# Low halves of loaded weights: the second operand of the subtraction moved from SBUF to a PSUM copy

## The chip, the cores and the metric

The kernel runs as one program on one core of a Trainium2 chip. The engines are named as the profile names them: PE is TensorE (PEld its weight loads), DVE is VectorE, ACT is ScalarE, POOL is GpSimd, SP is the engine whose queue issues most of the DMAs. The metric is the device time of one execution in microseconds. A profile describes one execution of its own, whose span is a few microseconds off the median of the timed runs.

## The reference

Two cross-attention layers with image tokens, over 16 sequences of 256 tokens and 320 channels (20 heads of 16). The context has 256 tokens of 512 channels; its last 4 tokens are image tokens. Cut to what matters (layer 0; layer 1 differs in how the image scores are normalised):

```python
q = x @ Wq;  k = text @ Wk;  v = text @ Wv
text_out = softmax(q_h @ k_h.T * scale) @ v_h
ip_k = ip @ Wk_ip;  ip_v = ip @ Wv_ip
fused = q_h @ ip_k_h.T * scale + 0.5 * sem          # sem: what the text attention reads, against ip
ip_out = (softmax(fused) * spatial_mask) @ ip_v_h
x = (text_out + ip_out) @ Wout + bout + x
```

Everything is float32. The kernel makes every product of two float32 matrices from a high half (the value rounded to the format that TensorE takes at full rate) and a low half (the value less its high half), and multiplies high by high, high by low and low by high.

## The kernel before, in words

The work runs in slots, one for each group of four heads of each sequence: 80 slots of layer 0 (five a sequence), then 80 of layer 1. A slot makes the scores (line 701 into the bank pair S), their row maxima on DVE (lines 702 and 703, tile `mn`), a turn of the maxima into rows by a small matmul (line 708) and a DMA, the transposed scores (line 723 into the banks T), their exponent on ACT (line 726, tiles `P`), a product with the image part on POOL (line 729), and the product with the values (line 766 into the bank P). In layer 1 the same places have lines 865, 867, 884, 859, 879, 895 (POOL), 904/905 (norms) and 916/926.

Between these, `fill` runs the steps of other tasks at set times: keys, queries, values, projections, and the loading of weights. The order of TensorE is the order in which the program is written; ACT, DVE, POOL and SP are ordered by the framework's scheduler, within limits that `queued` and `anchor` set.

What the change touches is `halves` (line 153): it rounds a source into `hi` with an ACT copy (line 158) and subtracts that from the source for `lo` (line 161), on DVE unless told otherwise. It is called with `loaded=True` for pieces that a DMA has brought into a raw tile in SBUF (`rawc` or `raw`, two buffers each), through `in_turn`. On DVE that is 31 pieces:

- the context of sequences 2 and 3, four pieces of 128x512 (`cta`, `ctb`), between 58 and 67 us of the span;
- the output weights of layer 0, three pieces of 128x320 (`wF`), from 85 to 99 us;
- the image tokens of all sequences, 128x256 (the `kst<-rawc` row), at 526 us, and the five weights of layer 1 that follow until 631 us: `wki1` (four `wB` pieces of 384), `wk1` (four of `wA`), `wv1` (four of `wC`, 320), `wvi1` (three `wB` of 512), `wq1` (three of `wE`, 384);
- the context of sequence 2 for layer 1 (two pieces of 512) at 722 us, and the output weights of layer 1 (three of 320) from 731 to 740 us.

A piece laid out by heads needs three subtractions (260, 4 and 60 columns, from `rounded`), an output weight two (256 and 64), the others one. The other contexts have their low halves made on POOL, and a source that TensorE made is in PSUM already; neither is touched.

`bank()` hands out the general PSUM banks, called X, in a ring of three, in the order in which the program asks for them. Whoever is given a bank waits until every reader of the tile that had it three requests earlier is done. `maxima0` (line 708), the projections, keys, values and semantic scores all take their banks from this ring.

Of the kernel before, what the change touches and what calls it, by code (L numbers as in the profile page):

```python
# [18 lines left out]
H = 20  # L19
HP = 24  # L20
D = 16
# [29 lines left out]
def xattn2(  # L51
# [27 lines left out]
    nc = tc.nc  # L79
# [11 lines left out]
    def bank(tag="X"):  # L91
        return ps.tile([128, 512], F32, tag=tag, name=tag, bufs=BANKS[tag])
# [60 lines left out]

    def halves(hi, lo, src, eng=nc.vector, loaded=False):
        order = queued if loaded else lambda inst: inst
        if len(hi.shape) != len(src.shape):
            src = src.rearrange("p (d h) -> p d h", d=D)[:, :, :H]
        order(nc.scalar.copy(hi, src))
        for to, *at in lo if isinstance(lo, list) else [(lo,)]:
            at = (slice(None), *at)  # L160
            order(eng.tensor_sub(to, src[at], f(hi)[at]))
# [22 lines left out]
    def in_turn(parts, wait, tag="raw", eng=nc.vector):  # L184

        ahead, parts, tags = [], list(parts), tag.split()
        for i in range(len(parts) + 1):
            if len(tags) > 1:
                new = () if i else range(len(parts))
            else:  # L190
                new = range(i + 1 if i else 0, min(i + 2, len(parts)))
            if i:
                halves(*ahead.pop(0), eng, wait)
            for j in new:
                src, hi, lo = parts[j]
                raw = buf(tags[j // 2 % len(tags)], [128, 512], bufs=2)
                shape = src.shape
                raw = raw[:, : shape[1]] if len(shape) == 2 else raw.rearrange("p (k n) -> p k n", k=shape[1])
                dma(raw, src)
                ahead.append((hi, lo, raw))  # L200
            if wait:
                yield
# [57 lines left out]
    def evacuate(hi, lo, out, m):  # L260

        if m < 2:
            return halves(hi, lo, out)
        hi, lo = hi[:64], lo[:64]
        both = buf("both", list(hi.shape), bufs=2)
        nc.scalar.copy(hi, out[:64])
        nc.scalar.copy(both, out[64:])
        nc.vector.tensor_sub(out[:64], out[:64], f(hi))
        nc.vector.tensor_add(lo, out[:64], both)  # L269
# [102 lines left out]
    def weights1():  # L372


        cipn = buf("rawc", [128, 512], bufs=2, name="cipn")[:BI]
        dma(cipn, cip_d)
        yield
        sq = buf("rawc", [128, 512], bufs=2, name="sq")[:BI]
        nrm = rn[:BI, 0:1]
        nc.scalar.activation(sq, cipn, AF.Square, accum_out=nrm)  # L380
        yield
        nc.gpsimd.tensor_scalar_max(nrm, nrm, EPS2)
        nc.gpsimd.memset(rn[:BI, 1:2], -0.5)
        nc.gpsimd.tensor_tensor(nrm, nrm, rn[:BI, 1:2], op=ALU.pow)
        yield
        dg = buf("rawc", [128, 512], bufs=2, name="dg")[:BI]
        nc.gpsimd.memset(dg[:, BI : BI + 128], 1.0)
        nc.scalar.activation(dg[:, :BI], ident[:BI, :BI], AF.Copy, scale=nrm)
        yield
        rp = bank()  # L390
        mm(rp[:, :BI], dg[:, BI : BI + 128], dg[:, :BI], start=True, stop=True)
        nc.vector.tensor_copy(rn, rp[:, :BI])
        cip = w1["cip"] = buf("kst", [128, 2, 4, BI], FR, bufs=SIZES["KST"], name="cip")
        raw = buf("rawc", [128, 4, BI], bufs=2, name="cipT")
        dma(raw, cipT_d.rearrange("(k p) n -> p k n", p=128))
        yield
        halves(cip[:, 0], cip[:, 1], raw, nc.vector, True)
        w1["loads"] = started(weights_by_row(wki1_d, 0.3, RAWS))
        yield
# [917 lines left out]
    for c in range(B // 2):  # L1317
        n, k = 10 * c, [("k0", c)] if c else []
# [14 lines left out]
    for b in range(B):  # L1333
        n = NS + 5 * b
# [340 lines left out]
```

## Time and profile before

| | |
|---|---|
| time, median of 3 runs | 1478.3 us (1476.85 to 1479.2) |
| time of the profiled execution | 1483.24 us |
| its span | 1481.5 us |
| busy: PE, POOL, DVE, ACT | 96%, 82%, 77%, 61% of the span |

"Busy" is the share of the span in which an engine had an instruction of its own running; an engine that waits for a semaphore is idle, but one whose instruction has been issued and is held up inside counts as busy. The page's second part cuts the span into 40 slices of 37 us; PE stands at 9 tenths nearly everywhere. The table of stretches gives the same for any stretch, with the clock that TensorE was granted (1.00 is full speed). In a row of the timeline, `x3` means that so many instructions were merged, and the brackets at its end hold the time for which the engine stood idle before the first, and what ended it.

### The profile page before, as it was taken

What the parts mean: (1) busy time and instruction counts of PE and PEld (TensorE: products, weight loads), DVE (VectorE), ACT (ScalarE), POOL (GpSimd) and SP (SyncE); (2) the same over time, 40 slices, a digit from 0 to 9 for tenths busy, and PEclk for the clock granted to TensorE, in tenths of its full rate; (3) what the DMA queues carried; (4) which work ended last, traced back from release to release, by engine and by line L of the source; (5) the groups of instructions that cost most, each with busy time, mean ns of one, the idle gap of its engine ahead of it and who ended that gap; (6) DMA issues with size and microseconds to landing.
All of it is one profiled execution on the core that took longest, in us unless ns stands there. A gap on an engine that the chain in (4) does not pass through costs nothing.

```text
span 1481.5 us, 35836 instructions
## 1 busy us (share of the span) xinstructions
PE 1418.0 (96%) x12578; PEld 1147.1 (77%) x12578; DVE 1133.5 (77%) x2527; ACT 897.5 (61%) x2173; POOL 1217.7 (82%) x1590
## 2 busy tenths in 40 slices
PE   8889999999999989789999999999999999999998
PEld 7778888888888878567778777877787777777765
DVE  6567777777777788867878888788878878887886
ACT  6346565656565645546666676666766766676663
POOL 6259898989999978889678888788878888888885
PEclk8899999999999999989999999999999999999999
DMA  7766777776777665765444444444444444533401
GB/s 241 199 205 202 214 209 214 204 213 193 229 205 219 201 202 160 198 201 157 138 105 124 126 135 110 125 140 120 116 119 138 121 116 120 147 114 93 125 25 51
DMA packets 229118, 232.43 MB, mean 157 GB/s; under 512 B 38186, under 2 KB 198860, under 8 KB 228940
## 3 DMA queue, kind: packets, MB, share of 16 engines
q1 hardware_dynamic: 226736, 229.18, 54.2%
q8 instruction: 100, 1.64, 0.5%
q10 hardware_dynamic: 2204, 0.97, 0.3%
q14 instruction: 78, 0.64, 0.1%
HBM read 117.65 MB, written 77.07 MB: 131 GB/s over the span
## 4 chain that ended last, share of the span: by engine, by line
PE 69%; POOL 10%; DVE 9%; DMA 4%; ACT 3%; issue 3%; SPq 1%; ACTq 0%; DVEq 0%; POOLq 0%
PE X L904 14%; PE X L247 14%; PE P L766 6%; PE X L567 6%; PE S L701 5%; PE P L916 4%; PE P L926 4%; PE T L723 4%; POOL wt L895 3%; PE T L859 3%; PE S L865 3%; POOL P L729 3%; PE X L257 2%; DMA qs<-qd 2%; PE X L570 1%
## 5 line engine op out<-in xcount | busy, mean ns | idle before, releaser
L729 POOL TENSOR_TENSOR P<-P,rs 128x512 f32<-128x512 f32 x320 | 408.1, 1304 | 80.4 <-ACT P L726 79.7
L895 POOL TENSOR_TENSOR wt<-P,ctb 128x512 f32<-128x512 f32 x316 | 402.4, 1293 | 39.8 <-ACT ctb L894 39.3
L904 PE MATMUL X<-ctb,gm 128*128 128x512 f32 x1106 | 295.4, 400 | 4.5 <-DVE wt L905 4.5
L726 ACT ACTIVATE P<-T 128x512 f32<-128x512 f32 x320 | 175.8, 594 | 178.7 <-PE T L723 135.3
L905 DVE TENSOR_TENSOR wt<-X,wt 128x512 f32<-128x512 f32 x320 | 217.3, 683 | 35.8 <-PE X L904 28.0
L904 PEld LDWEIGHTS X<-ctb,gm 128*128 128x128 f32 x1106 | 194.1, 189 | 39.1 <-DVE wt L905 7.9
L879 ACT ACTIVATE P<-T 128x512 f32<-128x512 f32 x320 | 173.2, 593 | 79.6 <-PE T L859 76.6
L894 ACT ACTIVATE ctb<-P 128x512 fp32r<-128x512 f32 x316 | 182.4, 626 | 14.9 <-PE X L904 13.6
L867 DVE TENSOR_REDUCE mn<-S 128x4 fp32r<-128x1008 f32 x160 | 191.2, 1195 | 0.0
L703 DVE TENSOR_REDUCE mn<-S 128x4 fp32r<-128x716 f32 x160 | 142.6, 891 | 0.0
L766 PE MATMUL P<-P,vr 128*32 128x256 f32 x1920 | 128.6, 390 | 2.7 <-POOL P L729 1.9
L701 PE MATMUL S<-ks,qs 125*128 125x256 f32 x640 | 118.1, 308 | 10.2 <-DVE mn L703 4.7
L701 PEld LDWEIGHTS S<-ks,qs 125*128 125x128 f32 x640 | 88.9, 195 | 46.9 <-issue 28.1
L723 PE MATMUL T<-qs,ks 127*128 127x256 f32 x640 | 106.0, 289 | 0.2 <-ACT P L726 0.2
L777 DVE STREAM_TRANSPOSE nt<-P 128x512 f32<-128x512 f32 x80 | 57.2, 715 | 52.2 <-PE P L766 51.3
L702 DVE TENSOR_REDUCE mn<-S 128x4 fp32r<-128x308 f32 x160 | 74.4, 465 | 28.5 <-PE S L701 28.2
L766 PEld LDWEIGHTS P<-P,vr 128*32 128x32 f32 x1920 | 56.2, 111 | 47.3 <-POOL P L729 7.7
L723 PEld LDWEIGHTS T<-qs,ks 127*128 127x128 f32 x640 | 90.6, 195 | 1.1 <-ACT P L726 0.6
L926 PE MATMUL P<-wt,zone 128*32 128x256 f32 x1280 | 85.3, 379 | 0.7 <-DVE wt L905 0.7
L916 PE MATMUL P<-P,v1t 128*32 128x256 f32 x1280 | 85.9, 385 | 0.0
L247 PE MATMUL X<-wC,cta 128*128 128x324 f32 (+1 forms) x480 | 79.9, 313 | 0.3 <-DVE kst L269 0.3
L865 PE MATMUL S<-ks,qs 48*128 48x256 f32 x640 | 74.5, 309 | 3.9 <-DVE mn L867 2.5
(389 smaller groups left out, 2999.3 us busy)
## 6 DMA issues: line engine op xcount, KB each, us to landing
qd<-q SPq DMA_DIRECT2D x96, 256.0 KB
qs<-tph SPq DMA_DIRECT2D x64, 308.0 KB
qs<-qd SPq DMA_DIRECT2D x80, 192.0 KB
ks<-kd SPq DMA_DIRECT2D x80, 192.0 KB
ks<-kd SPq DMA_DIRECT2D x160, 96.0 KB
qs<-qd SPq DMA_DIRECT2D x160, 96.0 KB
kd<-kst SPq DMA_DIRECT2D x57, 256.0 KB
ks<-M SPq DMA_DIRECT2D x64, 215.4 KB
```

The source lines that it names most:

```text
L247: last = mm(out, lhs(a, k), rhs(b, k), start=i == 0, stop=i == len(terms) - 1)
L701: mm(sp[:, h], Q[: XROW + T0, h, t * 128 : (t + 1) * 128], K[: XROW + T0, h], start=True, stop=True)
L723: mm(st[p][:, j], K[:KS0, 2 * p + j, t * 128 : (t + 1) * 128], Q[:KS0, 2 * p + j], start=True, stop=True)
L726: exp = anchor(nc.scalar.activation(pt, st[p], AF.Exp, scale=SCALE))
L729: anchor(nc.gpsimd.tensor_mul(pt, pt, rs[:, t : t + 1].to_broadcast([128, 2, S])))
L766: mm(pv[32 * s : 32 * s + 32, o : o + S], v[:, vt, h : h + 32], P[k, s // 2][:, t, s % 2], start=vt < 2, stop=vt != 1,)
L867: anchor(nc.vector.tensor_reduce(mn[:, :, t], sp[:, :, :T1], axis=AX.X, op=ALU.max))
L879: anchor(nc.scalar.activation(P[k, u][:, t], st[u], AF.Exp, scale=SCALE))
L894: nc.scalar.activation(R[k, u][:, t], P[k, u][:, t], AF.Copy, scale=0.5)
L895: anchor(nc.gpsimd.tensor_sub(W[k, u][:, t], P[k, u][:, t], f(R[k, u][:, t])))
L904: mm(yp, gm[:, gb], R[k, u][:, kt], start=i == 0, stop=i == len(blocks[n]) - 1)
L905: w1["wt"] = nc.vector.tensor_mul(W[k, u][:, n], yp, W[k, u][:, n])
```

## The change

For a loaded piece whose low half DVE makes, ACT first copies the whole raw piece into a general PSUM bank. The subtraction then reads that copy, and no longer the raw tile. The high half is still rounded from the raw tile in SBUF.

```diff
     def halves(hi, lo, src, eng=nc.vector, loaded=False):
         order = queued if loaded else lambda inst: inst
+        if loaded and eng is nc.vector:
+            n = 1
+            for d in src.shape[1:]:
+                n *= d
+            there = bank()[: src.shape[0], :n]
+            if len(src.shape) == 3:
+                there = there.rearrange("p (k n) -> p k n", k=src.shape[1])
+            order(nc.scalar.copy(there, src))
+        else:
+            there = src
         if len(hi.shape) != len(src.shape):
-            src = src.rearrange("p (d h) -> p d h", d=D)[:, :, :H]
+            src, there = [t.rearrange("p (d h) -> p d h", d=D)[:, :, :H] for t in (src, there)]
         order(nc.scalar.copy(hi, src))
+        src = there
         for to, *at in lo if isinstance(lo, list) else [(lo,)]:
             at = (slice(None), *at)
             order(eng.tensor_sub(to, src[at], f(hi)[at]))
```

ACT has 31 instructions more, and TensorE's order stays as it was. In the changed program the lines behind this place have numbers higher by 11: the new copy is line 163, the rounding 168, the subtraction 172.

DVE at the first piece of the output weights of layer 0, from the reciprocal of one slot on (`q_0` is the tile of the queries of the next sequence, `wF_0` the weight, `X_` a general bank). Before:

```order
L780 RECIPROCAL P_69<-nt_1_131 128x16
L161 TENSOR_TENSOR wF_0_998<-rawc_0_126,wF_0_998 128x256
L161 TENSOR_TENSOR wF_0_998<-rawc_0_126,wF_0_998 128x64
L781 TENSOR_TENSOR P_69<-P_69,mk_101 128x8
L161 TENSOR_TENSOR wF_0_998<-rawc_1_127,wF_0_998 128x256
L161 TENSOR_TENSOR wF_0_998<-rawc_1_127,wF_0_998 128x64
L161 TENSOR_TENSOR q_0_161<-X_972,q_0_161 128x256
L783 TENSOR_TENSOR tmp_1_818<-nt_1_131,P_69 128x256
L268 TENSOR_TENSOR X_983<-X_983,kst_0_182 64x2x179
```

After, on the same engine at the same place:

```order
L791 RECIPROCAL P_69<-nt_1_131 128x16
L792 TENSOR_TENSOR P_69<-P_69,mk_101 128x8
L794 TENSOR_TENSOR tmp_1_826<-nt_1_131,P_69 128x256
L172 TENSOR_TENSOR q_0_161<-X_980,q_0_161 128x256
L279 TENSOR_TENSOR X_991<-X_991,kst_0_182 64x2x179
L172 TENSOR_TENSOR wF_0_1006<-X_1024,wF_0_1006 128x256
L172 TENSOR_TENSOR wF_0_1006<-X_1024,wF_0_1006 128x64
```

The subtractions of the weight read a bank now, and the low half of the queries stands ahead of them, where it stood behind four of them.

ACT at the context of sequences 2 and 3, from its first piece to the maxima of slot 2 (`mt`) and their DMA. Before:

```order
L158 CAST cta_0_77<-rawc_0_126 128x512
L726 ACTIVATE P_0_122<-T_67 128x512
L726 ACTIVATE P_1_123<-T_68 128x512
L158 CAST cta_1_78<-rawc_1_127 128x512
L158 CAST ctb_0_79<-raw_693 128x512
L158 CAST ctb_1_80<-raw_695 128x512
L654 ACTIVATE rs_1_133<-X_755 128x512
L710 CAST mt_0_598<-X_767 16x128
L726 ACTIVATE P_2_124<-T_67 128x512
```

After:

```order
L163 COPY X_730<-rawc_0_126 128x512
L168 CAST cta_0_77<-rawc_0_126 128x512
L737 ACTIVATE P_0_122<-T_67 128x512
L737 ACTIVATE P_1_123<-T_68 128x512
L163 COPY X_763<-rawc_1_127 128x512
L168 CAST cta_1_78<-rawc_1_127 128x512
L168 CAST ctb_0_79<-raw_693 128x512
L168 CAST ctb_1_80<-raw_695 128x512
L163 COPY X_767<-raw_693 128x512
L665 ACTIVATE rs_1_133<-X_757 128x512
L163 COPY X_771<-raw_695 128x512
L721 CAST mt_0_598<-X_775 16x128
```

Four copies stand among the roundings and exponents, and the bank of the maxima, `X_775`, is the one that the copy `X_763` had.

ACT at the image values of layer 1 (`wvi1`), from an exponent to the maxima (`sp_1` holds the semantic scores of one half of a sequence, made by TensorE into a bank). Before:

```order
L726 ACTIVATE P_1_123<-T_68 128x512
L158 CAST wB_7664<-rawc_1_127 128x512
L158 CAST wB_7665<-rawc_0_126 128x512
L625 COPY sp_1_391<-X_7653 128x77
L710 CAST mt_0_598<-X_7677 16x128
```

After:

```order
L737 ACTIVATE P_1_123<-T_68 128x512
L163 COPY X_7711<-rawc_1_127 128x512
L168 CAST wB_7704<-rawc_1_127 128x512
L163 COPY X_7717<-rawc_0_126 128x512
L168 CAST wB_7705<-rawc_0_126 128x512
L636 COPY sp_1_391<-X_7693 128x77
L645 ACTIVATE sp_0_390,mx_0_394<-sp_0_390,mx_0_394 128x77
L721 CAST mt_0_598<-X_7721 16x128
```

Two copies stand ahead of the semantic scores, and the two banks that they take bring the bank of the maxima, `X_7721`, round to the one that these scores, `X_7693`, had.

## The prediction

> **What bounds the kernel now.** I read the page first, then the table of stretches, then TensorE's rows with the waits ahead of them, and last what DVE and POOL did in those waits.
>
> ```profile
> span 1481.5 us, 35836 instructions
> PE 1418.0 (96%) x12578; PEld 1147.1 (77%) x12578; DVE 1133.5 (77%) x2527; ACT 897.5 (61%) x2173; POOL 1217.7 (82%) x1590
> ...
> 57.00:70.00 13.00, 9.21 (x66) 6.54 (x65) 8.11 (x10) 5.40 (x12) 7.54 (x7) 0.85 0.78 198
> 83.00:95.00 12.00, 10.32 (x77) 9.41 (x79) 8.56 (x20) 5.45 (x14) 4.55 (x6) 0.86 0.75 228
> 520.00:635.00 115.00, 95.88 (x865) 78.89 (x865) 97.14 (x209) 60.11 (x151) 91.20 (x97) 0.96 0.66 183
> 718.00:745.00 27.00, 24.32 (x217) 18.54 (x210) 23.46 (x46) 16.09 (x37) 13.77 (x20) 0.94 0.47 143
> ...
> 745.00:1380.00 635.00, 631.40 (x5617) 492.41 (x5617) 515.48 (x1102) 427.34 (x1018) 530.97 (x818) 1.00 0.44 122
> ```
>
> A row of stretches gives its length, then PE, PEld, DVE, ACT and POOL busy, TensorE's clock, and the DMA's share and rate. TensorE is the bound: in 635 us of layer 1 it is idle for 3.6 us. The four stretches in which weights are loaded are the exception: of 167 us TensorE works 139.7, idle for 27.3 us, and its clock is below 1 in all four. Only there can the change win.
>
> Why, the clearest case shows:
>
> ```profile
> 526.23 4.24 DVE L161 TENSOR_TENSOR kst<-rawc,kst 128x256 fp32r<-128x256 f32 x1
> 526.44 2.53 POOL L729 TENSOR_TENSOR P<-P,rs 128x512 f32<-128x512 f32 x2
> 528.93 1.26 POOL L556 TENSOR_TENSOR ho<-hT,ho 128x512 fp32r<-128x512 f32 x1
> 531.50 0.23 PE L708 MATMUL X<-ident_r,mn 128*16 128x128 f32 x1 [2.68 <-DVE kst L161]
> ```
>
> A subtraction of 256 columns with both operands in SBUF lasts 4.24 us and ends at 530.47, just behind the third of three POOL instructions (530.19); DVE was held for as long as POOL kept going. TensorE stood for 2.68 us behind it.
>
> **What DVE gets back.** The first two rows give the time of everything that touches `rawc`, and `raw`, summed over the load stretches; DVE's part is the 59 subtractions. The next four are subtractions that no POOL work met, the last those with a PSUM operand.
>
> ```profile
> sum 160.00, PE 0.43 PEld 0.29 DVE 32.74 ACT 10.05 POOL 0.00; mean PE 0.05 PEld 0.04 DVE 4.09 ACT 1.26 POOL 0.00
> sum 160.00, DVE 14.67 ACT 5.01 POOL 0.00; mean DVE 1.83 ACT 0.63 POOL 0.00
> ...
> 549.08 0.62 DVE L161 TENSOR_TENSOR wB<-raw,wB 128x260 fp32r<-128x260 f32 x3
> 87.08 0.55 DVE L161 TENSOR_TENSOR wF<-rawc,wF 128x256 fp32r<-128x256 f32 x2
> 593.45 0.47 DVE L161 TENSOR_TENSOR wC<-raw,wC 128x320 fp32r<-128x320 f32 x1
> 722.20 1.28 DVE L161 TENSOR_TENSOR cta<-rawc,cta 128x512 fp32r<-128x512 f32 x2
> ...
> L161 DVE TENSOR_TENSOR q<-X,q x62: 411/425/427, 32.8 to 1372.8; 128x256 fp32r<-128x256 f32 x62
> ```
>
> Now 32.74 + 14.67 = 47.4 us. Unheld: 11 pieces of 384 at 0.62 (6.8), six of 320 in two parts at 0.55 (3.3), four of 320 at 0.47 (1.9), nine of 512 at at most 0.68 (6.1), one of 256 at 0.41 (0.4): 18.5 us. That a PSUM operand leaves DVE unheld, the last row shows: 62 subtractions all over a run in which POOL is 82% busy, none over 0.427 us. So DVE gets 28.9 us back; the bounds are 0 (still held) and 28.9, and I take 28.9 because the row is the same instruction.
>
> [...]
>
> **What of that TensorE gets back.** These are its waits in the load stretches (with the one at 531.50), two DVE rows behind them, and one stretch.
>
> ```profile
> 63.68 0.56 PE L247 MATMUL X<-ctb,wA 128*128 128x156 f32 x3 [1.11 <-DVE ctb L161]
> 66.58 0.71 PE L247 MATMUL X<-ctb,wA 128*128 128x156 f32 x2 [2.34 <-DVE ctb L161]
> 88.02 0.77 PE L247 MATMUL X<-cta 128*77 128x192 f32 x6 [1.36 <-DVE q L161]
> 542.22 0.51 PE L567 MATMUL X<-ho,wF 128*128 128x256 f32 x2 [0.80 <-POOL ho L557]
> 576.29 0.22 PE L708 MATMUL X<-ident_r,mn 128*16 128x128 f32 x1 [1.75 <-DVE mn L703]
> 596.55 0.34 PE L623 MATMUL X<-kb,q 128*128 128x156 f32 x1 [1.07 <-DVE q L269]
> 601.61 0.22 PE L708 MATMUL X<-ident_r,mn 128*16 128x128 f32 x1 [1.51 <-DVE mn L703]
> 610.67 0.34 PE L642 MATMUL X<-ident,sp 128*77 128x128 f32 x1 [2.66 <-ACT sp L638]
> 626.15 1.50 PE L766 MATMUL P<-P,vr 128*32 128x256 f32 x24 [0.57 <-DVE tmp L783]
> 628.91 0.74 PE L701 MATMUL S<-ks,qs 125*128 125x256 f32 x4 [1.26 <-DVE mn L703]
> 632.37 0.23 PE L708 MATMUL X<-ident_r,mn 128*16 128x128 f32 x1 [2.24 <-DVE mn L703]
> 741.33 0.50 PE L865 MATMUL S<-ks,qs 48*128 48x256 f32 x4 [2.51 <-DVE mn L867]
> ...
> 571.51 2.58 DVE L161 TENSOR_TENSOR wA<-raw,wA 128x260 fp32r<-128x260 f32 x3 [1.11 <-ACT wA L158]
> 736.63 3.03 DVE L161 TENSOR_TENSOR wF<-rawc,wF 128x256 fp32r<-128x256 f32 x2 [1.38 <-ACT wF L158]
> ...
> 615.00:630.00 15.00, 10.97 (x102) 8.08 (x102) 13.04 (x26) 6.82 (x15) 15.00 (x15) 1.00 0.65 176
> ```
>
> Without the one that names POOL they sum to 21.1 us. By stage, with what is late next:
>
> - Context at 58 us (3.45): DVE's gain is eaten by ACT. The first piece lands at 58.9; four copies, four roundings, two exponents and one other stand in a row, 8 x 0.57 + 2 x 0.54 + 0.6 = 6.3 us, to 65.2. With a subtraction of 0.68 the last low half is there at 65.9 instead of 66.5. Take **0.7**.
> - `wF` (1.36): in the order shown above the queries' subtraction no longer stands behind four of the weight's. Take **1.2**.
> - Image tokens (2.68): 4.24 becomes 0.41, but POOL's rows end at 530.19 all the same, and the wait at 542.22 is for POOL. Take **1.7**.
> - `wk1` (1.75): 2.58 becomes 0.62 ahead of the reduction waited for. Take **1.6**. `wv1` (1.07): **0.7**.
> - `wvi1` (1.51 and 2.66): **0**, since the third order shown puts a new wait here (priced below).
> - `wq1` (4.07): three pieces shrink, but POOL works all 15 us of 615 to 630. Take **2.5**.
> - `wo1` (2.51): 3.03 becomes 0.55. Take **2.2**.
>
> That is 10.6 us. To it comes the clock:
>
> ```profile
> 88.00:93.40 5.40, 5.07 (x28) 4.79 (x29) 2.43 (x7) 0.84 (x3) 0.46 (x1) 0.69 1.03 302
> 526.00:536.00 10.00, 7.16 (x66) 5.71 (x64) 7.94 (x12) 3.38 (x10) 5.47 (x8) 1.00 0.66 202
> 632.80:636.20 3.40, 3.40 (x20) 3.17 (x23) 1.64 (x3) 1.42 (x4) 3.40 (x5) 0.50 0.75 203
> 741.00:745.40 4.40, 4.07 (x18) 3.59 (x19) 3.41 (x8) 1.31 (x4) 0.63 (x3) 0.61 0.47 146
> ```
>
> After the waits at 88, 632 and 741 TensorE runs at half clock for 3.4 us, 1.7 us lost each time, 5.1 in all; after the one at 531.50 it does not. Bounds 0 and 5.1; I take the middle, **2.5**. [...]
>
> **What it costs.** The trace has no ACT copy from SBUF into PSUM; the nearest rows are the roundings, SBUF to SBUF.
>
> ```profile
> 58.90 0.62 ACT L158 CAST cta<-rawc 128x512 fp32r<-128x512 f32 x1 [1.35 <-DMA rawc<-in_cT_dram]
> 601.14 1.13 ACT L158 CAST wB<-rawc 128x512 fp32r<-128x512 f32 x2
> ...
> L729 POOL TENSOR_TENSOR P<-P,rs 128x512 f32<-128x512 f32 x320 | 408.1, 1304 | 80.4 <-ACT P L726 79.7
> ```
>
> 31 copies at 0.62 at most are 19 us, on an engine that is idle for 80 of the 167 us. All hidden is 0, all on the path 19. A copy ahead of an exponent delays POOL, which waits for exponents 0.25 us a piece (80.4 over 320): a dozen such copies at 0.25 are 3 us, my value, near the lower end because ACT is half idle. The cover for the rest is this idle time. Queued behind a copy on ACT are exponents, evacuations of banks and the DMAs of the maxima; TensorE and POOL wait for those. For the shorter ring elsewhere I add 1 us. SP only sees raw tiles come free a little sooner, as ACT and no longer DVE is their last reader: 0. Sum: 10.6 + 2.5 - 4 = **9.1 us** less. The profiled execution took 1483.24 us and would take 1474.1; it stands 4.9 above the median, from which I subtract the same: **1469.2 us**.
>
> **Rivals.** *All waits go*: 21.1 + 5.1 less a few for ACT, about 24, so 1454; for it speaks that DVE is named in nearly every wait, against it POOL's full 15 us. *The gain goes to the next late engine*: TensorE comes sooner and waits for POOL or ACT; 1 us left, 1477. For it speaks the 82% of POOL, against it TensorE's near absence of idle time from 745 us on, with the same POOL load. *The ring* (slower): a copy takes one of three banks, and TensorE, in order, stands at its third request behind a subtraction or an evacuation. The place is `wvi1`: two copies, 1.13 us as the roundings, push the semantic scores back, and the bank of the maxima waits for their addition, so that TensorE goes on near 603.7 instead of 601.6, 2.1 us lost. If ten of the copies do that, 21 us go against 13.1: 1486. It decides from 13.1 / 31 = 0.42 us a copy on. Against it speaks that elsewhere products of a microsecond lie between the copies. *It doesn't do what it says*: DVE stays held and 4 us are added, 1482; the 62 rows speak against it.
>
> **How the numbers follow.** Forecast (1462 to 1475) 0.61; all waits 0.14; next engine 0.14; ring 0.09; not as said 0.02. A measurement of this kernel tells about 0.2%, 3 us, from no change. Faster takes the first two, 0.75; same the third, 0.14; slower the last two, 0.11. The range, 1458 to 1479, holds all of the first and third and about a third of the second; it leaves out most of 'all waits' and the slower ones.
>
> **What would show it.** Right: the subtractions sum to about 18.5 us, none much over 0.7; the waits at 531, 576, 632 and 741 shrink below half, and the half-speed stretches behind the last two go. Wrong: rows of line 172 that still end with POOL's; copies well over 0.62 us; TensorE's maxima (line 719) or norms waiting for line 172 or 637; or the same idle time now named POOL or ACT.

## The result and the profile after

| | before | changed |
|---|---|---|
| median, timed side by side | 1478.3 us of 5 runs (1474.32 to 1481.74) | 1468.9 us of 5 runs (1465.03 to 1472.39) |
| ratio, with its 95% interval | | 0.9929 (0.9905 to 0.9954) |
| profiled execution and its span | 1483.24, 1481.5 us | 1465.03, 1463.2 us |

The kernel became faster by 9.4 us, 0.6%, and the interval leaves out 1; forecast were 9.1. The profiled executions lie 18.2 us apart, because the one before is 4.9 us above its median and the one after 3.9 below: what the two traces show by stage is more than the change is worth, and the experiments have to say which part of it repeats.

The first lines of the page after give the span and the busy times:

```profile
span 1463.2 us, 35841 instructions
PE 1409.4 (96%) x12578; PEld 1139.1 (78%) x12578; DVE 1108.8 (76%) x2527; ACT 909.4 (62%) x2204; POOL 1211.6 (83%) x1590
```

The view of the cores gives the mean clock that TensorE was granted (0.983 in the profile of before):

```profile
core 0: 1463.2 us, clock 0.992
```

DVE is busy 24.7 us less, ACT 11.9 us more with its 31 copies, PE 8.6 us less. The groups of the changed subtraction (by line, tile and shape, with count, busy us, mean ns of one, and the idle time ahead) show why:

```profile
L172 DVE TENSOR_TENSOR cta<-X,cta 128x512 fp32r<-128x512 f32 x4 | 2.8, 691 | 2.5 <-ACT cta L168 2.4
L172 DVE TENSOR_TENSOR wF<-X,wF 128x256 fp32r<-128x256 f32 x6 | 2.5, 413 | 0.0
L172 DVE TENSOR_TENSOR wA<-X,wA 128x260 fp32r<-128x260 f32 x4 | 1.7, 428 | 2.2 <-ACT wA L168 1.5 <-ACT X L163 0.7
L172 DVE TENSOR_TENSOR kst<-X,kst 128x256 fp32r<-128x256 f32 x1 | 0.4, 425 | 0.2 <-ACT kst L168 0.2
```

The copies, by their source line (count, shortest, median and longest in ns, when, and in which shapes):

```profile
L163 ACT COPY X<-rawc x21: 392/482/606, 55.8 to 720.8; 128x320 f32<-128x320 f32 x8, 128x512 f32<-128x512 f32 x6, 128x384 f32<-128x384 f32 x6, 128x256 f32<-128x256 f32 x1
L163 ACT COPY X<-raw x10: 431/502/602, 59.9 to 614.0; 128x384 f32<-128x384 f32 x5, 128x512 f32<-128x512 f32 x3, 128x320 f32<-128x320 f32 x2
```

The subtraction of the image tokens, 4.24 us before, lasts 0.425; none of the 59 in this trace is over 0.693, though POOL is busy 83% of the time. Counted as the time in which one of the 59 ran, they take 18.7 us (47.3 before).

TensorE's main waits in the load stretches of the changed kernel (start, duration, line, and in brackets the idle time ahead and what ended it):

```profile
61.06 0.29 PE L719 MATMUL X<-ident_r,mn 128*16 128x128 f32 x1 [3.82 <-ACT rs L665]
85.39 0.73 PE L258 MATMUL X<-cta 128*77 128x192 f32 x6 [1.53 <-ACT both L278]
...
528.73 0.97 PE L578 MATMUL X<-ho,wF 128*128 128x256 f32 x6 [0.84 <-ACT mt L721]
562.54 0.22 PE L719 MATMUL X<-ident_r,mn 128*16 128x128 f32 x1 [0.37 <-ACT tph L656]
580.12 1.21 PE L578 MATMUL X<-ho,wF 128*128 128x256 f32 x8 [2.48 <-DVE xc L825]
589.64 0.29 PE L719 MATMUL X<-ident_r,mn 128*16 128x128 f32 x1 [2.12 <-DVE wB L172]
597.07 0.34 PE L653 MATMUL X<-ident,sp 128*77 128x128 f32 x1 [1.28 <-ACT sp L649]
617.82 0.22 PE L719 MATMUL X<-ident_r,mn 128*16 128x128 f32 x1 [1.00 <-DVE mn L714]
```

Gone or nearly gone are the waits for the image tokens (2.68), for `wk1` (1.75, now 0.37) and for the output weights of layer 1 (2.51; nothing over 0.23 is left there); those at the semantic scores (2.66, now 1.28) and at `wq1` (2.24, now 1.00) are halved. The wait at `wF` is not gone: 1.36 before, 1.53 now. New are 3.82 at the context, 2.48 ahead of 580 and 2.12 at `wvi1`.

TensorE executes the same instructions in the same order in both programs, so the span can be cut at the start of the same instruction in each trace. This table is worked out so (us; the head of a column says where the cut lies in the trace of before). "Changed, again" is a second profile of the changed kernel, "layer 0 only" the experiment whose layer 1 is as before.

| | context, 42 to 83 | `wF`, to 104 | image tokens, 515 to 545 | `wk1`, to 585 | `wv1` and `wvi1`, to 612 | `wq1`, to 645 | 700 to 745 |
|---|---|---|---|---|---|---|---|
| before | 40.8 | 21.1 | 30.0 | 40.0 | 27.0 | 33.0 | 45.0 |
| changed | 41.5 | 16.1 | 28.4 | 36.4 | 27.4 | 31.3 | 42.3 |
| changed, again | 38.0 | 16.4 | 29.1 | 36.3 | 27.9 | 31.3 | 42.5 |
| layer 0 only | 42.8 | 15.8 | 30.2 | 38.5 | 27.0 | 33.2 | 45.4 |

Read in pairs, layer 1 gained 1 to 2 us at the image tokens, 2 to 4 at `wk1`, lost up to 1 at `wv1` and `wvi1`, gained 2 at `wq1` and 3 at the output weights. The wait of 2.48 ahead of 580 lies in the stage of `wv1` and `wvi1`, which begins at 571 us in that trace.

### The profile page after: what moved, and what is told of

Its sections match the earlier page's. It is cut to its first block, busy times and chain, and to the rows that moved or that the text cites. A ratio compares the mean times of both kernels' runs of the same rounds, so it can differ in the third digit from the quotient of the medians.

```text
span 1463.2 us, 35841 instructions
## 1 busy us (share of the span) xinstructions
PE 1409.4 (96%) x12578; PEld 1139.1 (78%) x12578; DVE 1108.8 (76%) x2527; ACT 909.4 (62%) x2204; POOL 1211.6 (83%) x1590
## 4 chain that ended last, share of the span: by engine, by line
PE 78%; DVE 8%; POOL 4%; DMA 3%; ACT 3%; issue 2%; SPq 1%; ACTq 0%; DVEq 0%; POOLq 0%
PE X L915 16%; PE X L258 16%; PE P L777 7%; PE X L578 6%; PE S L712 6%; PE T L734 4%; PE P L927 4%; PE P L937 3%; PE S L876 3%; PE T L870 3%; PE X L537 2%; DVE mn L878 2%; PE X L268 2%; POOL P L740 2%; DVE wt L916 1%
## 5 line engine op out<-in xcount | busy, mean ns | idle before, releaser
L578 PE MATMUL X<-ho,wF 128*128 128x256 f32 x480 | 68.1, 283 | 9.4 <-ACT mt L721 5.0
```

## The experiments

Each row compares with the kernel before on the same chip. Four groups share a chip: e1 to e4, e5 to e8, e9 and e10, e11 and e12 (the 1477.73 of the first and the third group is a coincidence). Between groups the ratio with its interval is what can be compared.

| run | median, us | before beside it | ratio (95% interval) |
|---|---|---|---|
| e1, copy only | 1482.68 | 1477.73 | 1.0034 (1.0022 to 1.0047) |
| e2, high half in PSUM | 1467.88 | 1477.73 | 0.9944 (0.9923 to 0.9966) |
| e3, two stages as before | 1468.37 | 1477.73 | 0.9938 (0.9921 to 0.9955) |
| e4, column on ACT | 1466.85 | 1477.73 | 0.9933 (0.9917 to 0.9948) |
| e5, layer 0 only | 1477.05 | 1478.87 | 0.9995 (0.9971 to 1.0018) |
| e6, layer 1 only | 1467.84 | 1478.87 | 0.9924 (0.9894 to 0.9953) |
| e7, e2 and e4 together | 1464.98 | 1478.87 | 0.9900 (0.9874 to 0.9926) |
| e8, fourteen pieces | 1466.87 | 1478.87 | 0.9913 (0.9887 to 0.9940) |
| e9, the changed kernel again | 1467.38 | 1477.73 | 0.9933 (0.9910 to 0.9956) |
| e10, eleven pieces, with e7 | 1468.48 | 1477.73 | 0.9944 (0.9924 to 0.9963) |
| e11, e7 again | 1464.44 | 1475.52 | 0.9934 (0.9913 to 0.9955) |
| e12, e7 with layer 1 only | 1467.60 | 1475.52 | 0.9940 (0.9919 to 0.9961) |

**e1: the copy and its bank stay, the subtraction reads SBUF as before.**

```diff
-            there = bank()[: src.shape[0], :n]
+            spare = bank()[: src.shape[0], :n]
...
-            order(nc.scalar.copy(there, src))
-        else:
-            there = src
+            order(nc.scalar.copy(spare, src))
+        there = src
```

> The copy into PSUM stays, with its bank and its 0.6 us on ScalarE, but the subtraction reads the raw tile in SBUF again. Theory (the gain is DVE freed from waiting for GpSimd): the 59 subtractions sum to 40 us or more again, and the time is that of before plus the cost of the copies, 0 to 5 us slower than before. Rival 1 (the gain comes from the new order on DVE and ScalarE, or from TensorE's clock, and not from the operand): the time stays within 3 us of the changed kernel, 9 us under before, whatever the subtractions last.

It is 4.95 us slower than before (3.3 to 6.9 by the interval). So the copies cost about 5 us when nothing reads them, and gain nothing. Two things e1 leaves open. At `wF`, and in part around `wvi1`, DVE keeps the order of before here, so a share of the new order in the gain is not excluded there; from 515 to 585 us the orders before and after differ in the place of seven instructions of DVE only. And a bank that is held until its subtraction is not priced, since nothing reads the spare one. Two of its groups on DVE:

```profile
L171 DVE TENSOR_TENSOR kst<-rawc,kst 128x256 fp32r<-128x256 f32 x1 | 4.0, 3961 | 0.2 <-ACT kst L167 0.2
L171 DVE TENSOR_TENSOR wE<-rawc,wE 128x260 fp32r<-128x260 f32 x2 | 3.9, 1950 | 0.2 <-ACT wE L167 0.2
```

and the wait of TensorE behind the first of them:

```profile
527.84 0.29 PE L718 MATMUL X<-ident_r,mn 128*16 128x128 f32 x1 [2.71 <-DVE kst L171]
```

The subtractions are held again (40.1 us in all, by the same count as the 18.7 above), and the 2.7 us at the image tokens are back.

**e2: the raw piece stays in SBUF, the rounded high half is copied into PSUM instead.**

Against the kernel before:

```diff
         order(nc.scalar.copy(hi, src))
+        high = f(hi)
+        if loaded and eng is nc.vector:
...
+            high = bank()[: hi.shape[0], :n]
...
+            order(nc.scalar.copy(high, f(hi)))
         for to, *at in lo if isinstance(lo, list) else [(lo,)]:
             at = (slice(None), *at)
-            order(eng.tensor_sub(to, src[at], f(hi)[at]))
+            order(eng.tensor_sub(to, src[at], high[at]))
```

> The other operand goes to PSUM: ScalarE copies the rounded high half into the bank, and the subtraction is raw piece in SBUF less that copy. Theory (one operand outside SBUF is enough, whichever): subtractions of 0.43, 0.15 and 0.21 us as in the changed kernel, none longer than 0.7, and a time within 3 us of the changed kernel. Rival 2 (it is the raw tile, freed earlier for the next DMA, that gives the gain): here DVE is the last reader of the raw tile again, so half of the 9 us or more is lost.

Its interval covers the changed kernel's ratio. In the time the runs show no difference between the two operands, and that the raw tile is free sooner is not what pays. One expectation missed: a subtraction of `wC` lasts 1.70 us, of which e9 shows the cause. Its row for the image tokens, with `rawc` and a bank as operands:

```profile
L170 DVE TENSOR_TENSOR kst<-rawc,X 128x256 fp32r<-128x256 f32 x1 | 0.4, 421 | 0.6 <-ACT X L167 0.6
```

**e3: the context of layer 0 and `wvi1` as before, 24 pieces through PSUM.** A flag `psum` is handed down from `in_turn`:

```diff
-        if loaded and eng is nc.vector:
+        if loaded and psum and eng is nc.vector:
```

> As the changed kernel, but the context at 58 us and the three image value pieces (512 columns, about 590 us) subtract from SBUF as before; 24 of the 31 copies stay. Theory (at these two places the copies give TensorE new waits, 3.82 us at 61 and 2.12 us at 589, that eat what DVE gains): the time is 0 to 3 us under the changed kernel; the wait at 589 shrinks, and those seven subtractions last 1 to 1.8 us again. Rival (every freed subtraction counts): 2 to 4 us slower than the changed kernel.

No difference from the changed kernel that the runs can tell. In its trace the new waits of the two stages are gone or smaller (at `wvi1` 1.03 instead of 2.12), the subtractions are held again (up to 1.78 us), and the old waits are back:

```profile
65.61 0.71 PE L258 MATMUL X<-ctb,wA 128*128 128x156 f32 x2 [2.34 <-DVE ctb L172]
592.99 0.23 PE L719 MATMUL X<-ident_r,mn 128*16 128x128 f32 x1 [1.03 <-DMA raw<-in_wq_dram]
601.49 0.33 PE L653 MATMUL X<-ident,sp 128*77 128x128 f32 x1 [2.12 <-ACT sp L649]
```

So in these two stages the change swapped one wait for another of the same size.

**e4: the masked column of the image values on ACT.** The wait of 2.48 us ahead of 580 stands behind a DVE instruction that the change does not touch, a `tensor_scalar` of 128x20 elements with its operand in SBUF (line 468).

```diff
-            nc.vector.tensor_scalar_add(vcols(v, V1W)[:, 1, :, 16], vcols(v, V1W)[:, 1, :, 16], tmask[:, 2:3])
+            nc.scalar.activation(vcols(v, V1W)[:, 1, :, 16], vcols(v, V1W)[:, 0, :, 16], AF.Copy, scale=tmask[:, 2:3])
```

> As the changed kernel, but the column of ones that is scaled by a mask in the two value tiles of layer 1 (128x20, one SBUF operand) is made by ScalarE and not by a tensor_scalar on DVE. In the changed kernel these two DVE instructions last 1.11 and 2.37 us while GpSimd works without a pause, and TensorE waits 2.48 us just behind the second. Theory (this form is held by GpSimd too, and TensorE's wait is its consequence): the wait at 580 us falls under 0.5 us, and the time is 1 to 3 us under the changed kernel. Rival (the wait comes from the bank ring alone): the wait stays above 1.5 us and the time within 1 us.

The wait falls to 0.18, as the theory had it, and 0.92 appears at the next maxima (0.33 in the changed kernel). The stage of `wv1` and `wvi1`, in which both lie, takes 25.9 us by the cuts of the table, where the changed kernel took 27.4 and 27.9. The whole time does not show it: the ratio, 0.9933, is the changed kernel's (0.9929, and 0.9933 in e9).

```profile
581.09 1.20 PE L578 MATMUL X<-ho,wF 128*128 128x256 f32 x8 [0.18 <-DVE xc L825]
583.21 0.22 PE L719 MATMUL X<-ident_r,mn 128*16 128x128 f32 x1 [0.92 <-DVE q L280]
```

**e5 and e6: layer 0 alone (7 pieces) and layer 1 alone (24).** A counter `pieces[0]` numbers the loaded pieces in the order of the program:

```diff
-        if loaded and eng is nc.vector:
+        pieces[0] += loaded and eng is nc.vector
+        if loaded and eng is nc.vector and pieces[0] <= 7:
```

and `pieces[0] > 7` in the second.

> Only the seven pieces of layer 0 (context of sequences 2 and 3, output weights) go through the PSUM copy; the other 24 are subtracted from SBUF as before. Theory (the gain is the sum of the held subtractions' waits, stage by stage): the prediction's terms for this part are 0.7 + 1.2 us of waits, 0.9 of clock and about 1 of cost, so about 2 us less than before, 1476; the profile of the changed kernel said -4.3 us for it (context +0.7, output weights -5.0), 1473.5. Rival (the gain at the output weights in that profile was a chance of the clock, which falls behind some waits and not behind others): no change or slower, since the context alone has got longer, 1478 to 1479.

> Only the 24 pieces of the layer-1 load (from the image tokens on) go through the copy; the seven of layer 0 are subtracted from SBUF as before. Theory: prediction's terms 8.7 us of waits, 1.6 of clock, 3 of cost, about 7 us less than before, 1470.5; with the stage lengths of the changed kernel's profile (-1.7, -3.7, +0.4, -1.7, -0.1, -2.6) 9.4 less, 1468.5. If the two parts are independent, this gain and that of the run with layer 0 alone add up to the 9.4 us of the whole. Rival (TensorE gives time won in layer 0 back later, or a wait won here is only moved): the two sums miss 9.4 us by more than 4.

Layer 0 brings 1.8 us by the medians and 0.7 by the ratio, with zero well inside the interval: theory and rival of e5 do not part, and the 4.3 us of the profile lie at the edge of that interval. Layer 1 brings 11.0. Together that is 12.8 against 9.4, within the scatter of the two, so there is no sign that one gives the other's gain back. The 4 to 5 us that the two profiles show at `wF` were mostly the profiled execution of before: its clock was halved twice there, and e6, with this stage as before, takes 17.4 us for it, not 21.1.

**e7, e8, e9: e2 and e4 together; fourteen pieces; the changed kernel again.** e8 keeps the copy only where a held subtraction was seen with TensorE behind it:

```diff
+        if loaded and eng is nc.vector and (5 <= pieces[0] <= 8 or 13 <= pieces[0] <= 16 or pieces[0] in (24, 25, 26, 29, 30, 31)):
```

> The high half in PSUM (as in the second run) and the masked column of the values on ACT (as in the fourth) together. Theory: each was at or 1 to 2 us below the changed kernel, nothing in them meets, so 1465 to 1468. Rival (ACT is the next engine to be late; the column's ACT instruction and the copy of the high half, which stands behind its rounding, together push an exponent back): 1469 to 1472.

> Only 14 of the 31 pieces go through the copy: those at which before a subtraction was seen held until POOL stopped and TensorE waited behind it (output weights of both layers, image tokens, wk1, wq1). Theory (a copy costs 5 us / 31 = 0.16 us, and the other 17 pieces were not on TensorE's path): the 17 copies left out save 2.7 us and lose little, 1466 to 1468. Rival (any subtraction with both operands in SBUF is held when it meets POOL, so pieces left as they were lie behind POOL in turn, since the order around them has moved): 1470 to 1474, with rows of the SBUF subtraction of wB, wC or cta over 1.5 us.

> The changed kernel itself once more, so that it stands beside the next run on the same chip. From its first runs and those of its parts: 9.4 us below before (ratio 0.9929), 1466 to 1470. A second profile of the same program also shows what of its stage lengths repeats: the wait ahead of the maxima at wvi1 (2.12 us) and the one at the end of the context (3.82 us) are set by the order and must be there again within 0.5 us; the half-clock stretches ahead of 120 us need not.

e7 has the lowest ratio of all, e8 lies where its theory put it, yet neither interval parts from the changed kernel's. The rows that e8's rival named are there all the same (subtractions of `wB` up to 3.17 us, of `wC` up to 1.5), but the time it expected from them, 1470 to 1474, did not come. e9 repeats the changed kernel (ratio 0.9933 after 0.9929), and its profile repeats the waits at the context (3.39, before it 3.82) and at `wvi1` (2.58 and 2.12). It also shows the `tensor_scalar` held for much longer. DVE's rows, then POOL's, then TensorE's:

```profile
574.95 6.07 DVE L468 TENSOR_SCALAR v1t<-v1t,tmask 128x20 f32<-128x20 f32 x1
576.08 4.94 DVE L172 TENSOR_TENSOR wC<-X,wC 128x320 fp32r<-128x320 f32 x1
578.65 2.39 DVE L468 TENSOR_SCALAR v1t<-v1t,tmask 128x20 f32<-128x20 f32 x1
580.95 0.07 DVE L467 MEMSET v1t<- 128x20 f32 x1
...
575.97 5.00 POOL L740 TENSOR_TENSOR P<-P,rs 128x512 f32<-128x512 f32 x4
...
581.10 1.19 PE L581 MATMUL X<-hq,wE 128*128 128x256 f32 x5 [2.61 <-DVE v1t L468]
```

Two instructions that take 0.57 and 0.28 us in the kernel before end with POOL's four products at 581.0, and a subtraction with a PSUM operand between them ends there too. It seems to stand behind the held one rather than to be held itself: in e7, which has the column on ACT, the pieces of `wC` take 0.46 to 0.48 us. The 1.70 us of e2 are of this kind: that row ends at 582.38 with a `tensor_scalar` of 3.17 us.

**e10, e11, e12: eleven pieces, all of layer 1, with e7's other edits; e7 again; e7 with the 24 pieces of layer 1.** e10 and e12 differ from e7 in the condition alone (`pieces[0] == 8 or 13 <= pieces[0] <= 16 or pieces[0] in (24, 25, 26, 29, 30, 31)`, and `pieces[0] > 7`).

> Eleven pieces instead of 31 go through PSUM, all of layer 1 (image tokens, wk1, wq1, output weights), with the high half as the one in PSUM, and the masked column of the values on ACT. Theory (layer 0's seven pieces bring nothing, the nine that TensorE never waited for cost their copies, and the column's wait was real): at or below the run with both, 1463 to 1466, and 3 to 5 us below the changed kernel beside it. Rival (the gain of the run with both came from having every subtraction off POOL's way): 1467 to 1470, like the changed kernel.

> The kernel with the high half in PSUM and the masked column on ACT (all 31 pieces) once more, beside the next run. If its 1465.0 us (ratio 0.9900, interval 0.9874 to 0.9926) was no chance: 1463 to 1467 again, and 2 to 4 us below the changed kernel's three medians of 1467.4 to 1468.9. If it was: 1467 to 1469.

> The same, with only the 24 pieces of layer 1 through PSUM. It tells which of the 20 pieces that the run with eleven left in SBUF cost it 3.5 us against the run with both. Theory (the three pieces of wvi1: left in SBUF they last 1.78, 1.67 and 0.99 us there, and TensorE waits 4.04 us for the semantic scores behind them; the seven of layer 0 bring nothing): 1463 to 1467, like the run beside it, with the subtractions of wvi1 at 0.69. Rival (layer 0's pieces are what is missing): 1467 to 1470.

e10 missed its theory: 1468.48, as its rival said. Its trace shows `wvi1` held again, and TensorE behind it; first the group on DVE in e10,

```profile
L173 DVE TENSOR_TENSOR wB<-rawc,wB 128x512 fp32r<-128x512 f32 x2 | 3.5, 1730 | 0.0
```

then TensorE's wait in e10,

```profile
600.15 0.49 PE L654 MATMUL X<-ident,sp 128*77 128x128 f32 x1 [4.04 <-ACT sp L650]
```

and in e7 the wait that is left there, and the same subtraction:

```profile
592.70 0.23 PE L717 MATMUL X<-ident_r,mn 128*16 128x128 f32 x1 [1.73 <-DVE sp L635]
593.15 0.69 DVE L170 TENSOR_TENSOR wB<-rawc,X 128x512 fp32r<-128x512 f32 x1
```

The stage of `wv1` and `wvi1` takes 28.6 us in e10, and 23.5, 24.2 and 24.2 in e7, e11 and e12, so there the freed `wv1` and `wvi1` show. But e12 was to come out like e11 and missed: it lies 3.2 us above it, where its rival had it, with intervals that overlap. Its profile is longer from 104 to 515 us (415.7 us, against 413.0 in e7, 411.0 in e11 and 410.2 in the changed kernel), where DVE has no loaded piece. Which of the pieces make e10's difference in the whole time stays open.

So does whether e7 is better than the changed kernel. Its two medians, 1464.4 and 1465.0, are the lowest of all, 2 to 4.5 us below the changed kernel's two, but the ratios, 0.9900 and 0.9934 against 0.9929 and 0.9933, do not part. What repeats is one stage: in all four traces with the high half of `wvi1` in PSUM (e2, e7, e11, e12) TensorE's wait for the semantic scores, 1.28 in the changed kernel, is gone, and the stage takes 23.5 to 24.8 us, where e4 takes 25.9 and the changed kernel 27.4 and 27.9. e7 is the version I would keep, for this stage.

## Why the prediction came out right, point by point

**DVE's 28.9 us.** Right: 18.5 us were forecast for the 59 subtractions and 18.7 measured, and a PSUM operand freed them where POOL ran, in either operand (0.425 us at the image tokens in the changed kernel, 0.421 in e2, 4.24 before). The longer rows with such an operand that the text shows (1.70 in e2, 4.94 in e9) end with a `tensor_scalar` that is held ahead of them. The 0.41 us that the forecast takes for 256 columns is the first of the pair at 87.08 in the kernel before, which has both operands in SBUF and met no POOL work.

**The cost of the copies, 4 us.** Right within its error: 5 by e1 (3.3 to 6.9), in a kernel whose DVE is held. A copy lasts 0.39 to 0.61 us, as the roundings from which it was estimated.

**TensorE's 10.6 us and the clock's 2.5.** The sum was right; the split can only be estimated. Mean clock and span are listed with each run: before 0.9865 and 1475.8 us over 59 runs, the changed kernel 0.9901 and 1466.4 us over its 11. If the share below 1 is taken as time lost, that is 20.0 us and 14.5: **at most 5.5 of the 9.4 us are clock**. It is an upper estimate, since TensorE also waits while its clock is halved (it works for 3.16 of 3.40 us in the fourth row below): over the 59 runs, a microsecond more that is lost by this count goes with 0.6 us more of span. By that second estimate, about 3 us are clock and 6 are waits less copies, close to the 2.5 and 6.6 forecast; with e1's 5 us for the copies, the waits brought 9 to 11. In the stretches after, clock in the third column from the end, the old dips that the prediction counted are gone (first three rows), and half clock comes with the new waits at `wvi1` and at the context (last two; the context had a stretch of half clock before, too):

```profile
85.40:90.80 5.40, 5.40 (x57) 4.54 (x57) 3.44 (x9) 1.48 (x5) 0.00 (x0) 1.00 1.00 313
618.20:621.60 3.40, 3.40 (x41) 2.51 (x41) 2.07 (x4) 1.81 (x5) 3.40 (x4) 1.00 0.74 202
708.00:735.00 27.00, 26.25 (x236) 19.28 (x235) 22.75 (x53) 20.58 (x48) 17.36 (x26) 1.00 0.49 147
589.40:592.80 3.40, 3.16 (x21) 2.36 (x25) 2.68 (x8) 2.80 (x11) 2.19 (x11) 0.50 0.87 226
61.00:67.10 6.10, 6.04 (x37) 5.12 (x41) 2.51 (x5) 2.03 (x6) 2.94 (x3) 0.50 0.35 107
```

At `wvi1` the wait is 2.12 us long, and the half clock begins at 589.40, 0.24 us ahead of its end.

Which waits cost clock is not left to chance entirely. In each of the 14 traces, without the first 30 and the last 8 us, the stretches at 0.50 begin a whole number of steps of 3.413 us apart, within 1 ns, and last one, two or three such steps. If every trace is cut into these steps, all 42 steps at full clock in which PE was busy less than 40% of the time are followed by half clock, and of the 5640 with 60% or more, four are; in between it is 30 of 65. By these counts it matters how much of a wait falls into one step. Before the change, the wait of 2.24 us that ended at 632.37 lies whole in one, and the one of 2.68 that ended at 531.50 in two (PE busy is the first number behind the length):

```profile
526.90:530.31 3.41, 1.92 (x17) 1.72 (x15) 3.41 (x1) 0.83 (x2) 3.29 (x3) 1.00 0.32 58
530.31:533.73 3.42, 2.23 (x21) 1.86 (x25) 2.70 (x7) 0.26 (x1) 0.95 (x2) 1.00 0.66 212
629.36:632.77 3.41, 1.17 (x9) 0.88 (x8) 3.34 (x9) 2.22 (x5) 1.76 (x2) 1.00 0.41 129
```

Half clock follows the third of these rows and neither of the others.

**By stage.** Image tokens 1.7 (1 to 2 measured), `wk1` 1.6 (2 to 4, clock included), `wq1` 2.5 (2), output weights of layer 1 2.2 (3): right in place and order of size. (The list of waits leaves out three of 0.84, 1.04 and 1.17 us, at 540.45, 617.12 and 623.32; they stayed, at 0.84, 0.90 and 1.17.) The rest was wrong in its steps, with errors of both signs, so that a sum within 0.3 us is in part luck:

- Context, 0.7 gained: no gain shown (40.8 us before; 41.5, 38.0 and 42.8 in the three rows of the table with the copies). The step counted when DVE's last low half is ready, but the wait moved to the maxima, which need the bank of `rs`. ACT ran without a gap there, and `rs` stood behind three copies, of which one is shown, with another right behind it:

```profile
59.88 0.60 ACT L163 COPY X<-raw 128x512 f32<-128x512 f32 x1
60.40 0.60 ACT L665 ACTIVATE rs<-X 128x512 f32<-128x512 f32 x1
60.89 0.60 ACT L163 COPY X<-raw 128x512 f32<-128x512 f32 x1
```

- `wF`, 1.2 gained: the wait stayed (1.53, in place of 1.36). DVE's order changed as foreseen, but TensorE now waits for the second of two evacuations on ACT (`both`), with a copy of `wF` ahead of them:

```profile
84.13 0.42 ACT L163 COPY X<-rawc 128x320 f32<-128x320 f32 x1
84.58 0.36 ACT L277 CAST q<-X 64x256 fp32r<-64x256 f32 x1
84.97 0.37 ACT L278 COPY both<-X 64x256 f32<-64x256 f32 x1
```

  What went at this stage is a wait that the prediction's list leaves out, since it lies behind the stretch that was read. It stood in the kernel before at the maxima, behind the third piece of `wF`, held for 2.55 us:

```profile
96.38 2.55 DVE L161 TENSOR_TENSOR wF<-rawc,wF 128x256 fp32r<-128x256 f32 x2
100.18 0.23 PE L708 MATMUL X<-ident_r,mn 128*16 128x128 f32 x1 [2.06 <-DVE mn L703]
```

- `wv1`, 0.7 gained: its wait of 1.07 is gone, but the stage lost up to 1 us, with the wait at the masked column (below).
- `wvi1`, 0 gained with a new wait of 2.1: the size came (2.12 and 2.58 us in two profiles), but not by the chain forecast, so the size was luck. The text ahead of the prediction says that the banks go round strictly in threes, and that the maxima take the bank of the semantic scores. In the trace they do not: the maxima start at 589.64, and ACT reads the semantic scores only at 589.79 (line 636), so these still held their bank. By the releaser, the maxima had the bank of the first `wB` copy, and the wait ends with the copy's own subtraction (`wB` L172 in the row above), which is one of the signs that the prediction gave for being wrong. At the context, by the releaser again, they had that of `rs`, and not that of a copy, as the text ahead has it. A copy thus came between TensorE and a bank in these two places and at `wF`, and not in the ten of the rival "ring".

**Not foreseen** was the masked column at 580, an SBUF operand of DVE that the change left, which now comes upon POOL's work: 0.57 us at most before, 2.37 and 6.07 in the two profiles after.

**The signs of being right** came: the waits at 531, 576, 632 and 741 are at 0, 0.37, 1.00 and 0.17, and the half clock behind the last two is gone.

**The rivals.** "All waits go" (1454), "next engine" (1477) and "not as said" (1482) did not come. What TensorE got back was not handed on to POOL: in the two profiles of the changed kernel no wait that names it in the load stretches is over 0.9 us.

## What to carry to other kernels

Where DVE and GpSimd share a stretch, look for DVE rows that end with GpSimd's; one operand in PSUM, whichever is at hand, brought them back to their own length here (at the image tokens from 4.24 us to 0.425). Price the copies by a run that makes them and does not use them, and ask on its engine what now stands behind each copy: the waits at the context and at `wF` came from there, and the one at `wvi1` from the bank that a copy holds. After freeing the large operations, look for the small ones of the same kind that are left, since one held instruction stopped all that was behind it (in e9 the five that started on DVE between 576.08 and 577.81 all end at 581.02, with it). When you read what an edit did to a stage, first find the stage in which the wait lies.

## What the runs showed of the hardware

- A DVE subtraction of 256 columns with both operands in SBUF lasted 4.24 us beside GpSimd's products, and 0.425 beside them with one operand in PSUM. A `tensor_scalar` of 20 elements a partition, with its operand in SBUF, was held too: up to 2.37 and 6.07 us in the two profiles of the changed kernel, and 0.28 and 0.57 us in the kernel before.
- In such a hold the rows of the instructions behind grow as well (4.94 us for `wC` in e9, 0.46 to 0.48 in e7), so a long row need not be the instruction that is held.
- The granted clock fell to 0.50 in steps of 3.413 us that keep their beat through a trace, after each of the 42 steps in which PE was busy less than 40%. By the upper estimate above, a run loses 20.0 us to this before and 14.5 after, more than the change brings.
- The format of the halves against float32, in the profile of before: two matmuls of 128x256 on halves (line 1168) start 0.12 us apart at 1464.7, the two instructions of one float32 product of that size (line 1206) 0.21 us apart at 1465.4.
